# Scatters of one table in a two-layer transformer block: ordered behind the table's zeros instead of behind each other

## The chip, the cores and the metric

The kernel runs on one core of a Trainium2 chip. Time is what the device takes for one execution, in microseconds (us). Before the change it is 2133.94 us, the median of three runs (2133.84 to 2136.27). The program is built by a planner (the tile framework): the Python code names instructions in an order, the planner follows the reads and writes of tiles and tensors, decides in which order each engine issues its instructions, and places the semaphore waits.

## The reference, cut to what matters

Input x is (4, 1024, 128) in float32; it passes through two layers, each an attention-like part and a mixture of experts.

```
h = layernorm(x) * (1 + ca) + sa ;  x = x + ga * attention(h)       # layer 0: 16 heads, causal softmax
h = layernorm(x) * (1 + cb) + sb ;  x = x + gb * moe_top2(h)        # 8 experts, 2 per token
h = layernorm(x) * (1 + ca) + sa ;  x = x + ga * selective_scan(h)  # layer 1: state-space scan
h = layernorm(x) * (1 + cb) + sb ;  x = x + gb * moe_capacity(h)    # 8 experts, 512 places each
```

Both mixtures send a token to the experts that the router chose. The kernel does this with tables in device memory: rows of tokens are sorted by expert, an expert works on blocks of 128 rows, and results are fetched back by the same indices. Every token and choice has a row of its own in the table, so that two scatters never write the same row; unused rows have to be zero.

## The kernel before, in words

Tokens lie in 32 tiles of 128 (8 to a batch item b). Layer 0's attention runs in eight stages (b, c), c being one of two halves of the heads. A stage walks 8 query tiles i in the order 7, 0, 6, 1, 5, 2, 4, 3 (n = 0 to 7), each in four groups g of 32 queries: `probabilities` makes scores on TensorE (PE), subtracts the minimum on VectorE (DVE, line 567), exponentiates on ScalarE (ACT, line 580), takes the reciprocal of the sum (DVE, `den`, line 583) and scales by it on GpSimd (POOL, line 586). `turned` (line 595) then transposes these probabilities on PE, and `weighted` multiplies them by the values. Query tile i is transposed while tile n + 1 is made: `second_half`. POOL also zeroes the part over the diagonal (line 684) and adds the rotated halves of q and k (lines 537 and 545).

The layer-0 mixture of item b - 1 is put beside stages (b, 0) and (b, 1), in steps of Python generators. `sort_tokens` (stage (b, 0); two steps per group g from n = 2 on) norms, routes, computes each token's row (`placei`, DVE line 381), and then scatters 8 tiles times 2 choices = 16 tiles of 128 rows of 512 bytes into the table `f_in[b]`, named `blocks_in` in the profile (line 385). Stage (b, 1) runs `Blocks`: a load (line 407) brings three blocks, the experts' matmuls follow, results go to `blocks_out`, and `return_steps` gathers them (line 287). For the last item `sort_tokens` and `Blocks` run beside layer 1's scan, whose own chain is PE `pu` (spread), DVE `pu` (906), ACT `da` (908), DVE scan `h` (910), POOL `hc` (914), PE `py`. There are 16 steps m of this for each item, two `hc` each; `h` has 3 buffers.

Layer 1's mixture scatters 28 tiles into `xd` (`slots_in`, line 997), which the change leaves alone, and the last four tiles, in `dispatch_last`, as 8 scatters into the table `g_in` (line 1077). `last_experts` loads that one (line 1107).

All tables are filled with zeros at the start by transfers of SP's queue (line 491). Engines issue in order, and so do the queues of SP and POOL: an instruction that waits holds up everything behind it. A scatter is issued by POOL[...]. Since the rows of a scatter are not known when the program is built, the planner takes each for a write of the whole table: a scatter waits until the one before it into the same table has landed, and the load waits for the last. To choose what an engine does next, the planner runs its own model of time; of the instructions that are ready in it, the one written first in the Python code goes first.

Of the kernel before, what the change touches and what calls it, by code (L numbers as in the profile page):

```python
# [49 lines left out]
def adaln_two_layers(ctx: ExitStack, tc: tile.TileContext, I: dict, out: bass.AP):  # L50
    nc = tc.nc
# [10 lines left out]
    def load(pool, name, eng=nc.sync):  # L62
# [13 lines left out]
        out=causal, in_=causal, compare_op=ALU.is_ge, fill=NEG, base=0, pattern=[[-1, P]], channel_multiplier=1  # L76
# [219 lines left out]
            yield  # L296
        add()

    kept = {}

    hT0 = keep.tile([P, S + 3], F32, name="hT0")
    nc.gpsimd.memset(hT0[:, 0:3], 0.0)
# [28 lines left out]
    def sort_tokens(b, kept, pool, ps, tag, xtag="fxn"):  # L331


        xn = pool.tile([P, TB, D], F32, tag=xtag, bufs=1, name="fxn")
        yield from norm_steps(b * TB, TB, xn)
        hT = pool.tile([P, S], F32, tag=tag, bufs=1, name="fhT")
        yield from feature_steps(xn, hT, ps, modT[0][:, 4, b : b + 1], modT[0][:, 3, b : b + 1])
        pl = ps.tile([P, TB, NE], F32, tag="m", name="fpl")
        for t in range(TB):
            mm(nc, pl[:, t, :], hT[:, t * P : (t + 1) * P], f_gate)  # L340
        yield
        m1, m2, oh1, oh2 = yield from top2_steps(pl, sm)

        both = sm.tile([P, TB, NE], F32, tag="f_both", bufs=1, name="f_both")
        nc.vector.tensor_add(both, oh1, oh2)
        flat = both.rearrange("p t e -> p (t e)")
        pin = ps.tile([P, TB + 1, NE], F32, tag="m", name="fpin")
        pinf = pin.rearrange("p t e -> p (t e)")
        mm(nc, pinf[:, : TB * NE], before, flat, stop=False)
        for n in range(1, TB):  # L350
            mm(nc, pinf[:, n * NE : TB * NE], ones, flat[:, : (TB - n) * NE], start=False, stop=(n == TB - 1))
        mine = sm.tile([P, NE], F32, tag="f_mine", bufs=1, name="f_mine")
        nc.vector.tensor_reduce(mine, both.rearrange("p t e -> p e t"), AX.X, ALU.add)
        mm(nc, pin[:, TB, :], ones, mine)
        yield
        z = sm.tile([P, TB], F32, tag="f_z", bufs=1, name="f_z")
        nc.vector.scalar_tensor_tensor(z, m1, 1e-20, m2, ALU.add, ALU.add)
        nc.vector.reciprocal(z, z)
        w = keep.tile([P, 2, TB], F32, tag=f"f_w{b}", name="f_w")
        nc.vector.tensor_mul(w[:, 0], m1, z)  # L360
        nc.vector.tensor_mul(w[:, 1], m2, z)
        yield

        blocks, upto, which = yield from find_blocks(pin[:, TB, :], NB, sm)
        expert = keep.tile([P, NB], I32, tag=f"f_expert{b}", name="f_expert")
        nc.vector.tensor_scalar(expert, which, float(NE - 1), None, ALU.min)
        yield

        nc.vector.tensor_tensor(upto, upto, blocks, ALU.subtract)
        pos = sm.tile([P, TB, NE], F32, tag="f_pos", bufs=1, name="f_pos")  # L370
        nc.vector.scalar_tensor_tensor(
            pos, upto.unsqueeze(1).to_broadcast([P, TB, NE]), float(P), pin[:, :TB, :], ALU.mult, ALU.add
        )
        yield
        place = sm.tile([P, 2, TB], F32, tag="f_place", bufs=1, name="f_place")
        placei = keep.tile([P, 2, TB], I32, tag=f"f_placei{b}", name="f_placei")
        for k, oh in enumerate((oh1, oh2)):
            nc.vector.tensor_mul(oh, oh, pos)
            nc.vector.tensor_reduce(place[:, k], oh, AX.X, ALU.add)
            yield  # L380
        nc.vector.tensor_copy(placei, place)
        kept[b] = expert, placei, w
        for t in range(TB):
            for k in range(2):
                nc.gpsimd.indirect_dma_start(
                    out=f_in[b][:, :],
                    out_offset=bass.IndirectOffsetOnAxis(ap=placei[:, k, t : t + 1], axis=0),
                    in_=xn[:, t, :],
                    in_offset=None,
                )  # L390
                yield

    class Blocks:
# [9 lines left out]
        def load(self, n):  # L403
            rows_in = f_in[self.b].rearrange("(q p) d -> p q d", p=P)
            m = min(3, NB - 3 * n)
            self.xe = self.pool.tile([P, 3, D], F32, tag="fxe", name="fxe")
            nc.sync.dma_start(self.xe[:, :m], rows_in[:, 3 * n : 3 * n + m])

        def turn(self, n):

# [52 lines left out]
    with ExitStack() as es:  # L463
# [22 lines left out]

        for slots in f_in + xd + [g_in]:
            flat = slots.rearrange("(p r) d -> p (r d)", p=P)
            for at in range(0, flat.shape[1], 512):
                n = min(512, flat.shape[1] - at)  # L490
                nc.sync.dma_start(flat[:, at : at + n], mask[:, :n])

        def rotated(w, chunk, hT, dst):

# [242 lines left out]
    with ExitStack() as es:  # L737
# [273 lines left out]
        def dispatch_last():  # L1011
# [62 lines left out]
            yield  # L1074
            for t in range(nt):
                for k in range(2):
                    nc.gpsimd.indirect_dma_start(
                        out=g_in[:, :],
                        out_offset=bass.IndirectOffsetOnAxis(ap=placei[:, k, t : t + 1], axis=0),
                        in_=hx[:, t, :],  # L1080
                        in_offset=None,
                    )
                yield

            tiles = slice(t0, t0 + nt)
# [1 line left out]
                x[:, tiles, :], x[:, tiles, :], gate_bias[:, b : b + 1, :].to_broadcast([P, nt, D])  # L1087
            )

        sent = []  # L1090

        def last_experts():

            b, nb = B - 1, NLB
            expert = sent[0][0]
            rows_in = g_in.rearrange("(q p) d -> p q d", p=P)
            rows_out = g_out.rearrange("(q p) d -> p q d", p=P)
            ws, ins, xT, ye = {}, {}, {}, {}

            def load(j):  # L1100
                for r in range(j, min(j + 2, nb)):
                    ws[r] = load_block(eb, 6, "gw", "g_w", expert, r)

            def rows(q):
                n = min(4, nb - q)
                ins[q] = eb.tile([P, 4, D], F32, tag="gxe", name="gxe")
                nc.sync.dma_start(ins[q][:, :n], rows_in[:, q : q + n])

            def hidden(j):
                q = j - j % 4  # L1110
                if j == q:
                    n = min(4, nb - q)
                    tp = ps_m.tile([P, 4, P], F32, tag="m", name="gtp")
                    for r in range(n):
                        nc.tensor.transpose(tp[:, r], ins[q][:, r], ident)
                    xT[q] = eb.tile([P, 4, P], F32, tag="gxT", name="gxT")
                    shift, scale = modT[1][:, 3, b : b + 1], modT[1][:, 4, b : b + 1]
                    nc.vector.tensor_scalar(xT[q][:, :n], tp[:, :n], scale, shift, ALU.mult, ALU.add)
                    if q + 4 < nb:
                        rows(q + 4)  # L1120
                    ye[q] = eb.tile([P, 4, D], F32, tag="gye", name="gye")
                n = min(2, nb - j)
                ph = [ps_u.tile([P, NFC, P], F32, tag=f"pu{(j + r) % 4}", name="gph") for r in range(n)]
                act = eb.tile([P, 2, NFC, P], F32, tag="gact", name="gact")
                for r in range(n):
                    for f in range(NFC):
                        mm(nc, ph[r][:, f], ws[j + r][:, f * P : (f + 1) * P], xT[q][:, j - q + r])
                    nc.scalar.activation(act[:, r], ph[r], AF.Gelu_apprx_tanh)
                return j, n, act

            def results(j, n, act):
                q = j - j % 4
                py = ps_y.tile([P, 2, D], F32, tag="py", name="gpy")
                for r in range(n):
                    w = ws.pop(j + r)
                    for f in range(NFC):
                        w2 = w[:, NFC * P + f * D : NFC * P + (f + 1) * D]
                        mm(nc, py[:, r], act[:, r, f], w2, start=(f == 0), stop=(f == NFC - 1))
                nc.vector.tensor_mul(
                    ye[q][:, j - q : j - q + n], py[:, :n], gate_b1[:, b : b + 1, :].to_broadcast([P, n, D])  # L1140
                )
                if j + 6 < nb:
                    load(j + 6)
                if j > q or j + n == nb:
                    nc.scalar.dma_start(rows_out[:, q : j + n], ye[q][:, : j + n - q])

            rows(0)
            for j in range(0, 6, 2):
                load(j)
            made = None  # L1150
            for j in range(0, nb, 2):
                ahead = hidden(j)
                if made is not None:
                    results(*made)
                made = ahead
                yield
            results(*made)
# [274 lines left out]
```

## Time and profile before

| what | value |
|---|---|
| median of three runs | 2133.94 us |
| the profiled execution's own time | 2139.09 us |
| its span, first to last instruction | 2137.4 us |
| mean granted PE clock | 0.915 of full speed |
| PE busy | 1792.8 us (84%) |
| DVE busy | 1323.7 us (62%) |
| POOL busy | 994.6 us (47%) |
| scatters into `blocks_in` | 64, 986 ns each (median), from 490.2 us to 1581.5 us |
| scatters into `g_in` | 8, 957 ns each, from 1941.6 us to 1961.3 us |

A profile page gives each engine's busy time, then the same in forty slices, where a digit is the busy share in tenths. A view of one tile lists the instructions that touch it, with durations as least/median/most in ns, and for how long its engine sat idle before them and what ended that. A timeline gives start and duration of instructions in order; an idle time before an instruction stands in brackets with what ended it ("issue" where the profile shows nothing that was waited for). A view by stretches gives each engine's busy time between two moments, then PE's granted clock, the share of the DMA engines and GB/s.

### The profile page before, as it was taken

To read this page: it belongs to the slowest core of one execution; us is meant where nothing else is said; L and a number is where in the kernel's file an instruction comes from. 1 tells how busy PE (TensorE), PEld (TensorE's weight loads), DVE (VectorE), ACT (ScalarE), POOL (GpSimd) and SP (SyncE) were. 2 spreads that over 40 slices of the span, in tenths; PEclk is the share of its full clock that TensorE was granted. 3 is DMA by queue.
4 is the path that set the end of the run, shared out by engine and by line. 5 is a ranking of instruction groups with operands and counts; after the bars stand their busy time and mean duration, and the time that the engine had idled before them with its cause. 6 is when DMAs were issued, how large, how long until landed. Compare 5 with 4: busy or idle time off the path is not lost. (4 is left out here: it accounts for less than half of the span.)

```text
span 2137.4 us, 29054 instructions
## 1 busy us (share of the span) xinstructions
PE 1792.8 (84%) x8957; PEld 971.7 (45%) x8957; DVE 1323.7 (62%) x4000; ACT 947.3 (44%) x2073; POOL 994.6 (47%) x1277
## 2 busy tenths in 40 slices
PE   5399999998999989899989899967769757857984
PEld 3144344444455445455535446533335423325774
DVE  5356556665667666566766566655858888882243
ACT  1145454554445374355455454544456345423321
POOL 1334534436523643633363652344654675772254
PEclk9699999999999999999989999987979877867997
DMA  6400101001222200222210122210003230002345
GB/s 221 137 1 15 36 1 28 23 1 54 72 75 68 70 4 27 73 59 68 78 36 1 51 75 65 61 44 10 26 30 98 71 113 13 8 21 88 99 144 149
DMA packets 103756, 123.59 MB, mean 58 GB/s; under 512 B 15024, under 2 KB 68656, under 8 KB 103600
## 3 DMA queue, kind: packets, MB, share of 16 engines
q1 hardware_dynamic: 84256, 99.01, 15.7%
q0 software_dynamic: 8192, 16.74, 2.4%
q10 hardware_dynamic: 11152, 5.97, 0.9%
q8 instruction: 71, 1.16, 0.2%
q14 instruction: 85, 0.70, 0.1%
HBM read 67.85 MB, written 32.90 MB: 47 GB/s over the span
## 5 line engine op out<-in xcount | busy, mean ns | idle before, releaser
L586 POOL TENSOR_SCALAR pr<-pr,den 128x32 f32<-128x32 f32 (+31 forms) x512 | 353.2, 705 | 301.9 <-DVE den L583 295.9
L580 ACT ACTIVATE pr<-pr,nb 128x32 f32<-128x32 f32 (+31 forms) x512 | 371.6, 727 | 194.5 <-DVE nb L567 191.5
L595 PE MATMUL pt<-ident,pr 128*128 128x128 f32 x2304 | 341.9, 283 | 46.4 <-POOL pr L586 37.0
L46 PE MATMUL sc<-k,q 64*128 64x512 f32 (+14 forms) x1536 | 332.4, 525 | 41.4 <-DVE nb L567 24.4
L595 PEld LDWEIGHTS pt<-ident,pr 128*128 128x128 f32 x2304 | 253.8, 142 | 242.5 <-POOL pr L586 76.4
L46 PE MATMUL po<-pT,v 128*64 128x512 f32 x1152 | 345.9, 623 | 2.3 <-DVE pT L599 2.0
L597 ACT COPY pT<-pt 128x512 f32<-128x512 f32 x288 | 167.5, 582 | 356.8 <-PE pt L595 295.5
L567 DVE CUSTOM_DVE_ANT_0 pr<-sc,mask 128x512 f32<-128x512 f32 (+15 forms) x512 | 273.0, 559 | 76.2 <-PE sc L46 67.1
L599 DVE COPY pT<-pt 128x512 f32<-128x512 f32 x288 | 198.4, 689 | 166.1 <-PE pt L595 152.9
L46 PEld LDWEIGHTS sc<-k,q 64*128 64x128 f32 x1536 | 123.8, 193 | 197.6 <-DVE nb L567 93.3
L914 POOL TENSOR_TENSOR hc<-h,cc 128x512 f32<-128x512 f32 x128 | 161.6, 1275 | 108.7 <-DVE h L910 43.1
L46 PE MATMUL pu<-du,spread 128*128 128x512 f32 x256 | 146.4, 677 | 45.4 <-DVE h L910 41.0
L684 POOL MEMSET pr<- 128x288 f32 x128 | 42.4, 339 | 265.4 <-PE pt L595 261.3
L567 DVE CUSTOM_DVE_ANT_0 pr<-sc,mask,nb 128x416 f32<-128x416 f32 (+15 forms) x256 | 120.0, 496 | 7.0 <-PE sc L46 5.8
L908 ACT ACTIVATE da<-dt,negA 128x512 f32<-128x512 f32 x128 | 91.6, 719 | 66.1 <-DVE h L910 65.9
L46 PEld LDWEIGHTS po<-pT,v 128*64 128x64 f32 x1152 | 69.6, 136 | 84.4 <-issue 43.0
L503 DVE TENSOR_TENSOR rot_w<-proj,sin_sb 128x512 f32<-128x512 f32 x80 | 55.1, 688 | 76.7 <-PE proj L46 43.2
L906 DVE TENSOR_TENSOR pu<-pu,bb 128x512 f32<-128x512 f32 x128 | 85.2, 684 | 25.0 <-PE pu L46 14.9
L1300 POOL DMA_INDIRECT y<-slots_out,slot x56 | 56.5, 1009 | 93.8 <-PE ph L46 50.2
L46 PEld LDWEIGHTS pu<-du,spread 128*128 128x128 f32 x256 | 45.8, 207 | 115.4 <-DVE h L910 69.5
L545 POOL TENSOR_TENSOR q<-rot_u,rot_v 128x512 f32<-128x512 f32 x64 | 81.2, 1270 | 33.4 <-DMA rot_v<-rot_w 25.0
L580 ACT ACTIVATION_READ_ACCUMULATOR pr<-pr,nb 128x1 f32 x512 | 96.3, 188 | 0.0
(273 smaller groups left out, 2716.8 us busy)
## 6 DMA issues: line engine op xcount, KB each, us to landing
fw<-in_f_w SPq DMA_DIRECT2D x92, 320.0 KB
rot_v<-rot_w SPq DMA_DIRECT2D x320, 64.0 KB
gw<-in_g_w SPq DMA_DIRECT2D x15, 512.0 KB
fxe<-blocks_in SPq DMA_DIRECT2D x28, 192.0 KB
blocks_out<-fye SPq DMA_DIRECT2D x28, 192.0 KB
blocks_in<-mask SPq DMA_DIRECT2D x20, 256.0 KB
slots_in<-mask SPq DMA_DIRECT2D x16, 256.0 KB
g_w<-in_g_w SPq DMA_DIRECT2D x8, 512.0 KB
```

What stands on the lines that cost most here:

```text
L46: return nc.tensor.matmul(out, lhsT, rhs, start=start, stop=stop)
L545: nc.gpsimd.tensor_add(to, u.rearrange("p (n q) -> p n q", q=QG), v.rearrange("p (n q) -> p n q", q=QG))
L567: nc.vector.tensor_tensor_reduce(out=pr[hp][:, g, lo:hi], in0=sc[:, hp, : hi - lo], in1=mask[:, MW - hi + lo :] if hi == nk else mask[:, : ...
L580: nc.scalar.activation(p, p, AF.Exp, bias=nb[:, last, hp : hp + 1], scale=-1.0, accum_out=den[:, hp : hp + 1])
L586: nc.gpsimd.tensor_scalar(p, p, den[:, hp : hp + 1], 1.0, ALU.mult, ALU.mult)
L595: next_to(hp == 0 and g == 0, lambda: nc.tensor.transpose(to, p, ident))
L597: nc.scalar.copy(pT[:, hp, :], pt)
L599: nc.vector.tensor_copy(pT[:, hp, :], pt)
L906: nc.vector.tensor_mul(pu, pu, bb[:, tok])
L908: nc.scalar.activation(da, dt[:, tok], AF.Exp, scale=negA[:, c : c + 1])
L914: nc.gpsimd.tensor_mul(hcs[-1], h, cc[:, tok])
L1300: nc.gpsimd.indirect_dma_start(out=y, out_offset=None, in_=yd[k][:, :], in_offset=bass.IndirectOffsetOnAxis(ap=slot[:, k, t : t + 1], axis=0),
```

## The change

A function `scatter` now issues every scatter of `f_in[b]` and `g_in`. It keeps a list for each table. Its first entry is the name of a group; from the second scatter on, `declare_no_dep` takes away the waits for scatters that are in the group. Each scatter is then put into the group and given waits for the transfers that zero the table (`zeros`, six of them for an `f_in` table, four for `g_in`). `behind` gives each load of such a table a wait for every scatter into it, where before it waited for the last one. Computation, sizes, number of instructions and buffers are the same. The scatters into `xd` and all gathers are unchanged.

```diff
+    def after_all(ins, others, reason):
+        for other in others:
+            tc.add_manual_dep(ins, other.name,
+                mybir.DependencyInfo(mybir.DependencyClass.Sync, mybir.DependencyReason.DATA), reason=reason)
+
+    def scatter(group, out, at, in_, fill):
+        ins = nc.gpsimd.indirect_dma_start(
+            out=out, out_offset=bass.IndirectOffsetOnAxis(ap=at, axis=0), in_=in_, in_offset=None
+        ).ins
+        if group:
+            tc.declare_no_dep(ins, group=group[0], reason="different rows")
+        else:
+            group.append(f"rows of {ins.name}")
+        tc.add_to_no_dep_group(group[0], ins)
+        after_all(ins, fill, "zeros")
+        group.append(ins)
+
+    def behind(read, group):
+        after_all(read.ins, group[1:], "scattered rows")
...
         for t in range(TB):
             for k in range(2):
-                nc.gpsimd.indirect_dma_start(
-                    out=f_in[b][:, :],
...
+                scatter(arrived[b], f_in[b][:, :], placei[:, k, t : t + 1], xn[:, t, :], zeros[b])
...
-            nc.sync.dma_start(self.xe[:, :m], rows_in[:, 3 * n : 3 * n + m])
+            behind(nc.sync.dma_start(self.xe[:, :m], rows_in[:, 3 * n : 3 * n + m]), arrived[self.b])
...
         for slots in f_in + xd + [g_in]:
+            zeros.append([])
...
-                nc.sync.dma_start(flat[:, at : at + n], mask[:, :n])
+                zeros[-1].append(nc.sync.dma_start(flat[:, at : at + n], mask[:, :n]).ins)
...
-                    nc.gpsimd.indirect_dma_start(
-                        out=g_in[:, :],
...
+                    scatter(came_in, g_in[:, :], placei[:, k, t : t + 1], hx[:, t, :], zeros[-1])
...
-                nc.sync.dma_start(ins[q][:, :n], rows_in[:, q : q + n])
+                behind(nc.sync.dma_start(ins[q][:, :n], rows_in[:, q : q + n]), came_in)
```

More of the change, by code (lines that the diff above doesn't have):

```diff
@@ L297, in return_steps @@
         add()
-    kept = {}
+    def after_all(ins, others, reason):
+        for other in others:
+            tc.add_manual_dep(
+                ins,
+                other.name,
+                mybir.DependencyInfo(mybir.DependencyClass.Sync, mybir.DependencyReason.DATA),
+                reason=reason,
+            )
+    def scatter(group, out, at, in_, fill):
[11 more added lines that the diff above has]
+        after_all(read.ins, group[1:], "scattered rows")
+    kept, arrived, zeros = {}, {}, []
     hT0 = keep.tile([P, S + 3], F32, name="hT0")
@@ L382, in sort_tokens @@
         kept[b] = expert, placei, w
+        arrived[b] = []
         for t in range(TB):
             for k in range(2):
-                nc.gpsimd.indirect_dma_start(
-                    out=f_in[b][:, :],
[L387 to L390, printed above, removed]
+                scatter(arrived[b], f_in[b][:, :], placei[:, k, t : t + 1], xn[:, t, :], zeros[b])
                 yield
@@ L1076, in dispatch_last @@
                 for k in range(2):
-                    nc.gpsimd.indirect_dma_start(
-                        out=g_in[:, :],
[L1079 to L1082, printed above, removed]
+                    scatter(came_in, g_in[:, :], placei[:, k, t : t + 1], hx[:, t, :], zeros[-1])
                 yield
@@ L1088, in dispatch_last @@
             )
-        sent = []
+        sent, came_in = [], []
         def last_experts():
```

## The prediction

> **What bounds the kernel now.** I read the page first: shares, slices, and the chain that ended last.
>
> ```profile
> span 2137.4 us, 29054 instructions
> ...
> PE   5399999998999989899989899967769757857984
> ...
> POOL 1334534436523643633363652344654675772254
> PEclk9699999999999999999989999987979877867997
> ```
>
> PE is full through layer 0's attention (from the third slice to the 26th), so a microsecond in which PE stands there is a microsecond of the end. POOL is half idle: its own waits cost only where PE waits for POOL. The view of the table `blocks_in`, and then that of `g_in`, says what the scatters wait for:
>
> ```profile
> L385 POOL DMA_INDIRECT blocks_in<-fxn,f_placei x64: 966/986/1476, 490.2 to 1581.5; - x64
> ...
>   DMA blocks_in<-fxn,f_placei: 47.7, 34
>   issue: 4.5, 27
> ```
> ```profile
>   DMA g_in<-hx,g_placei: 13.0, 7
> ```
>
> So the waits that the change takes away are 47.7 us in 34 pieces, and 13.0 us in 7. By the timeline of POOL they lie in four windows of 16 scatters (from 490, 837, 1178 and 1530 us: 12.3, 13.3, 12.2 and 9.9 us) and one of 8 (from 1941 us). What they cost PE is read from the same place on both engines, here the second window; first POOL, then PE, then the view by stretches (length, then busy times of PE, PEld, DVE, ACT, POOL; clock):
>
> ```profile
> 864.99 0.98 POOL L385 DMA_INDIRECT blocks_in<-fxn,f_placei  x1 [1.16 <-DMA blocks_in<-fxn,f_placei]
> 867.50 0.97 POOL L385 DMA_INDIRECT blocks_in<-fxn,f_placei  x1 [1.54 <-DMA blocks_in<-fxn,f_placei]
> 868.49 1.28 POOL L537 TENSOR_TENSOR k<-rot_u,rot_v 128x512 f32<-128x512 f32 x1
> 869.72 1.52 POOL L586 TENSOR_SCALAR pr<-pr,den 128x608 f32<-128x608 f32 x2
> ```
> ```profile
> 870.56 0.48 PE L595 MATMUL pt<-ident,pr 128*128 128x128 f32 x1 [5.80 <-POOL pr L586]
> ```
> ```profile
> 524.00:530.00 6.00, 6.00 (x17) 3.25 (x17) 1.12 (x4) 0.00 (x0) 4.37 (x5) 0.62 0.07 22
> ...
> 871.00:876.00 5.00, 4.71 (x17) 2.55 (x15) 1.44 (x4) 0.00 (x0) 4.25 (x6) 0.77 0.06 21
> ```
>
> The scaling of width 608 is late because POOL spent its time waiting for scatters to land: its `den` was there at 863.4 us (DVE, 863.17 + 0.17), it ran at 869.7. PE stood for 5.80 us, and afterwards ran at 0.77 of its clock for 5 us. The first and third windows show the same at the same scaling: 6.47 us (to 523.96) and then 0.62 for 6 us; 4.83 us (to 1221.54) and then 0.71 for 5 us.
>
> **The change part by part.**
>
> *Waits of the three attention windows.* A landing takes 2.51 us from one issue to the next where nothing lies between (`g_in`, 1944.15 to 1946.65), and 0.96 of it is the instruction, so 1.55 us is saved a time. A rule would make it less: the Trainium skill, "DMA: Bandwidth & Descriptors", section on the anatomy of a GpSimd DMA, has 2.0 us fixed plus bytes over 436e3 a us; 64 KB give 2.15, less 0.96 is 1.19 (an estimate from that page), or 40 us for 34 waits. The trace has 47.7 and I take that.
>
> POOL then has to do all its work without gaps. The price of a scatter is not zero: twelve gathers in a row (2070 to 2085 us) take 1.30 us apiece, 1.00 and 0.30 of issue, and scatters into `slots_in` between other work 1.01 and 0.17. What matters is how much earlier the scaling 608 comes. Window 2: from the first scatter (837.5) 10.1 us of waits lie before it and 12 scatters; if the other 4 now also go ahead of it that costs 4 x 1.3 = 5.2, and denser issue about 1.0 more: 3.9 us earlier, PE's stall 5.80 becomes 1.9. If they don't go ahead, `den` is the limit and the whole 5.80 is gained. Window 1: 10.8 - 5.2 - 1.0 = 4.6 of 6.47. Window 3: 14 scatters are ahead already, 12.2 - 2.6 - 1.2 = 8.4, more than the stall, so 4.83. I take the lower ends, 4.6 + 3.9 + 4.8 = 13.3.
>
> *The clock.* After the three stalls PE lost 6 x 0.38 + 5 x 0.23 + 5 x 0.29 = 4.9 us of full-speed time. By the skill, "TensorE: Matmul & The Clock Gate", Part 1, the clock halves after an idle window of some 3.4 us and a window of activity raises it: that would be 3 x 1.7 = 5.1 us lost now. It also says that stalls cut to 1.9 us are safe, which no row here shows; by the row alone I could claim only a share equal to that of the stall removed (13.3 of 17.1, 3.8 us). I take 4.9. Attention: -18.2 us. PE is full right afterwards (1.00 of 1.00 busy from 537 to 560), so this goes through to the end.
>
> *The fourth window* is another matter. POOL was itself the bound from 1530.1 to 1551.4: 9 `hc` of 1.27 (11.4 us), 8 scatters, some 2.2 us of waits, and PE's `py` waits for the last `hc` (5.28 us, 1551.40). By the code all 16 scatters stand at steps m up to 12, and POOL is at m = 12 to 15 by then: freed, all are overdue, and are taken before the `hc`. Then 16 x 1.29 + 11.4 = 32.1 us instead of 21.3: +10.8. Against it: the 7 scatters that now follow to 1581 are out of the way, and PE may do the next item's inputs (`p`, `pd`, ready from 1547, done at 1559) before `py`, at best -10. The nearest row is the trace's own bunch:
>
> ```profile
> 1748.10 0.95 POOL L287 DMA_INDIRECT fy<-blocks_out,f_placei  x1 [0.30 <-issue]
> 1749.07 3.70 POOL L914 TENSOR_TENSOR hc<-h,cc 128x512 f32<-128x512 f32 x3
> ```
> ```profile
> 1744.94 2.08 PE L46 MATMUL pu<-du,spread 128*128 128x512 f32 x2 [13.26 <-DVE h L910]
> ```
>
> Sixteen overdue gathers from 1728.07 to 1749.05 went ahead of `hc` whose `h` was done by 1730.5, and PE stood for 13.26 us. There was less other work for PE than at 1551. Nearer to the upper end, I take +4.
>
> *`g_in`*: 0. POOL has nothing from 1962.3 to 2012.5, PE is full of slot experts, and the table's blocks are first transposed at 2065.5; the load was issued at 1963.6. Without that 100 us of cover its 13.0 us would count in full. SP's order could put the load before an `xe` load; with four `xe` buffers ahead that is within -0 and +1. I take 0.
>
> *New waits*: zeros landed by some 70 us, 420 us before the first scatter: 0; uncovered they would be one landing, 2.5 us. Loads wait for 16 scatters: semaphore instructions on SP of 17 to 28 ns (26 of them for these loads now), at most seven more a table, 5 x 7 x 0.028 = 1 us on SP's queue. Behind them wait the rotations (`rot_v`), POOL's additions of q after those; the first load is needed at 554.4 and goes out at 543.8, so 0, up to +1 if it blocks `rot_v` at the wrong moment. The load cannot be later: the last scatter is earlier. Transfers in flight together: 16 x 64 KB in 21 us are 50 GB/s, where the last slices carry 149: 0.
>
> **Sum**: -18.2 + 4 = -14.2. The profiled execution took 2139.09 (span 2137.4, 1.7 around it), 5.1 above the median; on the span 2123.2, on the median 2133.94 - 14.2 = **2119.7 us**.
>
> **The rivals.**
>
> *The burst (slower).* The planner is free to issue scatters as soon as `placei` is there, and POOL works in order: where its model shows an idle moment, it puts scatters ahead of scalings that on the chip are ready. A burst of 8 ahead (10.3 us) delays the scalings of n = 5 in windows 1 and 2 to about 505 (500.6 + 4.7; PE needs them at 503.8: +1.5 each) and in window 3 the scaling 736 to 1190.8 (PE got it at 1187.35: +3.5). That makes -18.2 + 6.5 + 10.8 = -1: this is the point from which it decides. With all 16 ahead, PE stands 11.8, 11.8 and 13.8 us longer there, -18.2 + 37.4 + 10.8 = +30. At 12, half way, +15: 2149 us. For it: the bunch at 1728, and POOL idle for 2.56 us right before the first scatter at 1178.75. Against: the scalings of n = 5 stand ahead of scatters 4 to 15 in the code, and were ready in a row (x3 between scatters), so the planner takes them first.
>
> *Hidden (same).* PE's order is new everywhere, another producer (`den` behind `rot_w` on DVE, at 875.46 now) ends the same stall, the fourth window costs 10.8: -18.2 halved and +10.8, 2135.6 us.
>
> *The waits stay.* If the declaration did not reach the scatters, the time would be 2133.9. All pieces are in the code; little speaks for it.
>
> **How the numbers follow.** Gain as summed 0.58 (its own range 2107 to 2129, from full stalls and -10 in the fourth window to half the attention gain); burst 0.25 (2138 to 2164); hidden 0.14; waits stay 0.03. No change means within 0.2%, 4.3 us, about what a measurement of this kernel can tell. Faster 0.58; hidden and stay, less a part of hidden that ends above, 0.16; slower 0.26. The range reaches over both signs: 2107 to 2150 leaves out one in ten of the burst's upper part and about as much below.
>
> **What would show it.** The view of `blocks_in` and `g_in` has no idle time behind their own DMA. The scaling 608 follows its `den` at once, and the three PE stalls of 4.8 to 6.5 us shrink below 2 with the clock at 1.00 behind them; spans of the three windows fall from 50, 49 and 48 us to about 44 for the same matmuls. In the scan, 16 scatters stand in a row at 1.29 us before the last `hc`, and `py` is later than its neighbours on PE. It would be wrong if scalings (line 586) ready for long stand behind rows of scatters in the attention windows, or if other stalls have appeared outside the five windows from a new order of all engines.

## The result, and the profile after

The changed kernel takes 2149.24 us (median of 4, 2148.12 to 2151.59), the kernel before on the same chip 2135.11 us (median of 4, 2133.84 to 2139.17). The ratio is 1.0064, with a 95% interval of 1.0047 to 1.0082: slower by 0.6%, where 0.7% less had been forecast. (The number lies just inside the range of 2107 to 2150 us, which the slow rival had widened; the forecast was a gain.) The profiled execution took 2151.59 us, its span is 2149.9 us (before: 2137.4).

The waits did go. First the views of the two tables `blocks_in` and `g_in` after the change (of 64 and 8 scatters). Their own landing does not appear any more among what POOL was idle for; 47.7 us and 13.0 us stood there.

```profile
L311 POOL DMA_INDIRECT blocks_in<-fxn,f_placei x64: 967/972/1213, 491.1 to 1556.7; - x64
...
  issue: 16.4, 60
...
who waited for it (us, times):
  ACT fxn L172: 7.5, 1
```
```profile
L311 POOL DMA_INDIRECT g_in<-hx,g_placei x8: 957/962/962, 1953.8 to 1962.6; - x8
...
  DVE g_placei L1096: 4.8, 1
  issue: 2.1, 7
```

(L311 is the scatter, now in the function `scatter`; other lines of the file moved by 24 or so: 586 is 610, 684 is 708, 914 is 938.) The first view's last line is new: an activation on ACT waits 7.5 us for scatters.

The page's mean clock is 0.915, as before, and PE is busy 84% of the span, as before. So the loss has to be looked for in who waits for whom. What PE waited for, before and then after (us in total, times, longest):

```profile
PE pu L46 <- DVE h L910: 41.0, 25, 13.3
PE pt L595 <- POOL pr L586: 37.0, 38, 6.5
PE py L46 <- POOL hc L914: 30.7, 14, 9.3
PE sc L46 <- DVE nb L567: 24.4, 51, 1.8
PE pt L595 <- ACT pT L597: 5.4, 10, 1.4
```

```profile
PE py L46 <- POOL hc L938: 45.8, 16, 10.1
PE sc L46 <- DVE nb L591: 28.6, 51, 4.5
PE pu L46 <- DVE h L934: 28.4, 23, 6.9
PE pt L619 <- POOL pr L610: 23.5, 36, 5.7
PE pt L619 <- ACT pT L621: 11.6, 11, 6.1
```

PE does wait 13.5 us less for the scalings on POOL, nearly the 13.3 us that the prediction subtracted, and 12.6 us less for `h`. But it waits 15.1 us more for `hc`, 6.2 us more for the copies `pT` on ACT, and 4.2 us more for `nb`. The timeline of POOL in the second window tells why:

```profile
849.87 0.59 POOL L610 TENSOR_SCALAR pr<-pr,den 128x384 f32<-128x384 f32 x1
851.19 1.05 POOL L311 DMA_INDIRECT blocks_in<-fxn,f_placei  x1 [0.17 <-issue]
...
861.48 0.97 POOL L311 DMA_INDIRECT blocks_in<-fxn,f_placei  x1 [0.30 <-issue]
862.43 0.36 POOL L708 MEMSET pr<- 128x288 f32 x1
```

Nine scatters stand in a row, from 851.19 to 862.45 us, ahead of a memset of 0.36 us. That memset zeroes the part over the diagonal of the probabilities of the next query tile. Two instructions on DVE and PE answer to it:

```profile
862.83 0.28 DVE L591 CUSTOM_DVE_ANT_0 pr<-sc,mask,nb 128x64 f32<-128x64 f32 x1 [4.71 <-POOL pr L708]
```
```profile
864.68 2.08 PE L46 MATMUL sc<-k,q 64*128 64x512 f32 x4 [4.53 <-DVE nb L591]
```

The masked pass of DVE writes into what the memset clears, so it waits 4.71 us, and PE waits 4.53 us behind it. The first window has the same row of nine, 502.13 to 513.40; there PE's stall behind DVE is 1.70 us, and 2.15 us more follow. The scaling of width 608, which the prediction wanted 4.6 us earlier there, starts at 524.83 us, 1.7 us *later* than before (523.13), though no scatter has been waited for.

In the third window six scatters go ahead of the scalings of width 768, and then ACT's normalization of the scan's first item, which before ran behind the last scatter of this window, has been put between the copies of this window, some 19 us earlier. Its destination is the buffer `fxn` that the scatters still read. PE first, then ACT, after and before:

```profile
1192.91 1.36 PE L619 MATMUL pt<-ident,pr 128*128 128x128 f32 x5 [5.67 <-POOL pr L610]
...
1210.87 1.97 PE L619 MATMUL pt<-ident,pr 128*128 128x128 f32 x8 [6.11 <-ACT pT L621]
```
```profile
1209.47 0.88 ACT L172 ACTIVATE fxn<-x,ln_away,ln_r 128x128 f32<-128x128 f32 x2 [7.52 <-DMA blocks_in<-fxn,f_placei]
```
```profile
1228.75 0.50 ACT L172 ACTIVATE fxn<-x,ln_away,ln_r 128x128 f32<-128x128 f32 x1
```

In the scan, twelve scatters in a row run from 1536.27 us until 1551.35, then one `hc`, four more scatters, and the other eight `hc`. PE's `py` waits 10.09 us for the first of them; the same matmuls before (second view) stood behind nothing. The 5.28 us that the prediction read at 1551.40 stood before a later `py`, which now runs at 1567.77 without a wait:

```profile
1552.70 1.94 PE L46 MATMUL py<-hc,gather 128*32 128x512 f32 x8 [10.09 <-POOL hc L938]
```
```profile
1535.50 1.07 PE L46 MATMUL py<-hc,gather 128*32 128x512 f32 x8
```

Matching the same matmuls in both traces, the changed kernel stands at +0.2 us before the first window, +3.4 behind it (first expert block), +2.8 at the routing of the second item, +1.3 behind the second window, +8.5 at the end of layer 0, +6.2 at the start of the scan, +13.0 at the last table `g_in` and +12.5 at the end. There are two losses, of about 7 us in the third window and about 7 us in the scan, and no gain in the first two windows.

### The profile page after: what moved, and what is told of

Same layout as the page of the kernel before. It is cut to its first block, busy times and chain, and to the rows that moved or that the text cites. A ratio compares the mean times of both kernels' runs of the same rounds, so it can differ in the third digit from the quotient of the medians.

```text
span 2149.9 us, 29066 instructions
## 1 busy us (share of the span) xinstructions
PE 1798.7 (84%) x8957; PEld 966.8 (45%) x8957; DVE 1332.7 (62%) x4000; ACT 948.2 (44%) x2073; POOL 995.8 (46%) x1277
## 5 line engine op out<-in xcount | busy, mean ns | idle before, releaser
L46 PE MATMUL sc<-k,q 64*128 64x512 f32 (+14 forms) x1536 | 337.4, 531 | 47.4 <-DVE nb L591 28.6
L46 PE MATMUL pu<-du,spread 128*128 128x512 f32 x256 | 154.6, 710 | 43.1 <-DVE h L934 28.4
```

Source lines behind the costliest of these rows:

```text
L46: return nc.tensor.matmul(out, lhsT, rhs, start=start, stop=stop)
```

## The experiments

The theory after this reading: the freed waits are worth what was forecast, but a freed scatter may also be *issued* at another place, and the planner put rows of scatters ahead of short POOL instructions that others need, and changed the order of the other engines with it (**order**). The first rival: sixteen transfers of one table under way together are slow, or their writing disturbs others (**in flight**). The second: each window pays for something else, as the buffer `fxn` or the longer list of waits of a load. Times of one batch share a chip: for the first four runs the kernel before has there a median of 2122.97 us, for the next four 2123.04, for the next three 2121.57, for the last 2135.49. Ratios are compared, not times; the expectations in us were written for the kernel before at 2134. Traces of another chip compare with that of before only roughly. The kernel with `g_in` alone issues everything on PE, DVE, ACT and POOL in the order of before and keeps all other waits, yet its trace stands at -7.6 us at the end of layer 0 and at -16.4 at the last table; the one with the scan's table alone and the order kept, unchanged in layer 0, stands there at +0.6.

### The two halves of the change apart

One kernel has the change's waits, with all engines' instructions held to the order that they had before, by constraints on the order of issue that place no semaphore. The other has the order of the changed kernel and the waits of before.

```diff
+    free = {i.name for g in [*arrived.values(), came_in] for i in g[1:]}
+    for steps in ast.literal_eval(zlib.decompress(base64.b85decode(ORDER)).decode()).values():
+        last, among = None, []
+        for n in itertools.accumulate(steps):
+            ins = nc.find_inst_by_name("I-%d" % n)
...
+            for to in ([] if ins.name in free else among) or [last]:
+                if to is not None:
+                    tc.add_manual_dep(ins, to,
+                        mybir.DependencyInfo(mybir.DependencyClass.NoSync, mybir.DependencyReason.DATA),
+                        reason="order of issue")
```

(`ORDER` lists the instructions of the kernel before, engine by engine. In the second kernel it lists those of the changed one, put into the code of before.)

> The change's waits (scatters behind the zeros only), but every engine issues its instructions in the order of the kernel before; only neighbouring scatters may swap. Order theory (the loss is the planner's new order, the freed waits by themselves are a gain): about 2117 us, since the three stalls of PE at the scaling of width 608 (17.1 us) shrink to a few us, and about 2 us go in the scan. In-flight theory (several scatters under way at once are slow by themselves, in POOL's issue or in landing): 2135 us or more. Nothing-to-gain theory (POOL's waits were hidden, PE finds another wait at once): 2130 to 2138 us.

> The waits of the kernel before (each scatter behind the one before it), but every engine in the order of the kernel after. Order theory: clearly slower than the kernel after, since rows of up to 12 scatters that stand ahead of POOL's other work now take 2.5 us apiece instead of 1.3: 2170 to 2220 us. In-flight theory: no slower than the kernel after, 2149 us or less.

The order kept: 2100.59 us, ratio **0.9892** (0.9876 to 0.9907). The new order with the old waits: 2203.83 us, ratio **1.0370** (1.0355 to 1.0385). With the waits of the change alone the kernel is 1.1% faster; by the order of the change alone it is 3.7% slower. In the traces PE, DVE, ACT and POOL do issue in the order that was to be held. The gain is larger than the 2117 us expected (0.992); the loss lies within the 2170 to 2220 us. The two don't add up: the order costs 3.7% with the old waits and less without them. From the order kept to the change is 1.0064 - 0.9892 = 1.7%, some 37 us, which is the price of the order once the waits are gone. The view of `blocks_in` with the order kept (its scatters are line 418 there, since the list of the order takes lines):

```profile
L418 POOL DMA_INDIRECT blocks_in<-fxn,f_placei x64: 963/982/1212, 488.8 to 1554.0; - x64
...
  issue: 11.9, 57
...
DMA to landing us min/median/max: 2.2/2.4/8.1
```

No waits for the table's own transfers here either; the median from issue to landing is 2.4 us. With the old waits, where only one is under way, it is 2.3 us. (This view counts the table's loads and zeros too; for the 64 scatters alone it is 2.3 and 2.2 us.) So a landing is not slower, and the kernel is faster. Nor are sixteen under way: at one scatter every 1.28 us and 2.3 us to land, it is about two at a time, in a long row too. In flight falls for such rows as this order has; in the changed kernel's own trace the landings of these scatters are not recorded, but with rows of five (a run below) the median is 2.3 us as well.

### The tables apart

> Only the three tables scattered beside attention are freed; the fourth and g_in keep their waits. By the two traces, layer 0 ends 6 to 8 us later than before: order theory 2140 to 2143 us. If the loss came from the scan or from new order elsewhere: 2133 to 2136 us. My prediction's sum for these windows: 2117 us.

> Only the table scattered beside the scan is freed. The step of my prediction (16 overdue scatters go ahead of the hc) put it at +4, between -10 and +10.8; by the two traces the first scan item ends 4.4 us later and the rest of the scan adds 2: 2139 to 2142 us. If all the loss is in attention: 2134 to 2136 us.

> Only g_in is freed, the other four tables wait as before. GpSimd's 13.0 us of waits there go; the prediction had 0 us for it because 100 us of other work cover it: ratio 1.000 (0.999 to 1.001). If the landing of g_in were on the path after all, 0.994 to 0.998.

```diff
         if group:
-            tc.declare_no_dep(ins, group=group[0], reason="different rows")
+            if fill is not zeros[-1] and fill is not zeros[B - 1]:
+                tc.declare_no_dep(ins, group=group[0], reason="different rows")
```

(This is the edit for the attention tables; for the scan's table alone the condition is `fill is zeros[B - 1]`, for `g_in` alone `fill is zeros[-1]`. All three leave the order to the planner.) The three attention tables alone: 2129.64 us, 1.0021 (1.0003 to 1.0039). The scan's table alone: 2134.90 us, 1.0050 (1.0038 to 1.0063). `g_in` alone: 2122.30 us, 1.0007 (0.9996 to 1.0017). The first two add up to 0.71%, which is the change's 0.64% within the intervals. `g_in` is worth nothing, as forecast, although its waits are gone. Neither part gains when the planner orders it anew. In us the first was expected at 2140 to 2143 (1.003 to 1.004), which its interval meets; the second at 2139 to 2142 (1.002 to 1.004), which it exceeds.

### The same two parts with the order kept

> The order of before held on every engine, and only the three attention tables freed: the prediction's term for the attention windows by itself, with the scatters where it had them. The prediction said -18.2 us, which is 0.9914 of 2123. If the first experiment's gain (0.9892) is the sum of the attention windows and of the fourth one, with the share that the sixth run leaves for the fourth: 0.9925 (0.991 to 0.9945). If all of the gain is in the attention windows: 0.989.

> The order of before held on every engine, and only the scan's table freed: 2.2 us of GpSimd's waits lie before the last hc there, 7.7 us behind it. If the loss of the fourth experiment (1.005) is the order's and not the table's, this is faster than before: 0.9965 (0.995 to 0.9985). If the freed table costs whatever the order, 1.003 to 1.006; if it is hidden, 1.000.

```diff
         if group:
-            tc.declare_no_dep(ins, group=group[0], reason="different rows")
+            if fill is not zeros[-1] and fill is not zeros[B - 1]:
+                tc.declare_no_dep(ins, group=group[0], reason="different rows")
```

(This stands beside the block of the first experiment, which holds the order of every engine; for the scan's table the condition is again `fill is zeros[B - 1]`.) The attention tables: 2104.54 us, **0.9913** (0.9892 to 0.9934). The scan's table: 2121.56 us, **0.9995** (0.9981 to 1.0009). The expectation of 0.9965 for the scan's table missed: there the gain of the waits is hidden. A cost of holding the order as such does not show either. So the attention tables are worth 0.87% in the old order and cost 0.2% in the planner's; the scan's is worth nothing in the old one and costs 0.5% in the planner's. The second window of POOL with the attention tables free and the order kept (scalings are line 718 here, memsets 816):

```profile
850.13 1.47 POOL L718 TENSOR_SCALAR pr<-pr,den 128x576 f32<-128x576 f32 x2 [0.64 <-DVE den L715]
851.77 1.06 POOL L418 DMA_INDIRECT blocks_in<-fxn,f_placei  x1 [0.17 <-issue]
852.82 0.64 POOL L816 MEMSET pr<- 128x288 f32 x2
853.63 0.98 POOL L418 DMA_INDIRECT blocks_in<-fxn,f_placei  x1 [0.17 <-DMA rot_v<-rot_w]
854.92 0.97 POOL L418 DMA_INDIRECT blocks_in<-fxn,f_placei  x1 [0.30 <-DMA rot_v<-rot_w]
855.91 1.29 POOL L669 TENSOR_TENSOR k<-rot_u,rot_v 128x512 f32<-128x512 f32 x1
857.16 1.53 POOL L718 TENSOR_SCALAR pr<-pr,den 128x608 f32<-128x608 f32 x2
```

Scatters stand one or two between the others' instructions, the scaling 608 runs at 857.16 us (before: 869.72), and POOL now waits for `den`, not the reverse. The stretches around the scaling, in the columns of the prediction's view (length, busy times of PE, PEld, DVE, ACT, POOL, then the clock), first before, then the change, then attention tables free and order kept; in each the second line is the third window. They are the same stretches of time, not quite of work: by the third window the last kernel is some 14 us ahead.

```profile
845.00:877.00 32.00, 25.34 (x123) 12.49 (x119) 15.49 (x51) 10.03 (x23) 21.35 (x27) 0.89 0.15 42
1183.00:1223.00 40.00, 32.35 (x166) 16.33 (x165) 19.54 (x66) 17.92 (x45) 26.78 (x36) 0.94 0.12 35
```
```profile
845.00:877.00 32.00, 27.48 (x134) 13.28 (x131) 14.53 (x47) 11.31 (x24) 24.25 (x31) 0.89 0.19 56
1183.00:1223.00 40.00, 28.14 (x132) 14.85 (x134) 13.05 (x45) 16.42 (x43) 24.54 (x34) 0.79 0.11 34
```
```profile
845.00:877.00 32.00, 29.39 (x130) 12.58 (x130) 20.14 (x59) 13.19 (x32) 24.43 (x29) 1.00 0.26 68
1183.00:1223.00 40.00, 37.86 (x184) 17.69 (x182) 25.20 (x72) 18.70 (x44) 25.97 (x33) 1.00 0.22 59
```

In the order kept PE is busy for 29.39 of 32 us and for 37.86 of 40, at 1.00 of its clock in these stretches. In the change PE gains 2 us in the second window at the same clock of 0.89, and loses 4 us and 0.15 of clock in the third.

### What in the order costs: POOL, the others, the buffer, the number in flight

Only POOL's order kept: the block of the first experiment, with a list of POOL's instructions alone.

```diff
+    for steps in ast.literal_eval(zlib.decompress(base64.b85decode(ORDER)).decode()).values():
```

> The change's waits with only GpSimd's order held to that of before; the other engines get whatever order the planner then gives them (TensorE's differs from before in 433 places). If GpSimd's order alone is the cause, most of the first experiment's gain comes back: 0.989 to 0.994. If the new order of the other engines costs by itself: 0.998 to 1.006.

The scatters of the attention tables in the program's order, the other two tables as before:

```diff
-        ins = nc.gpsimd.indirect_dma_start(
+        dma = nc.gpsimd.indirect_dma_start(
...
-            tc.declare_no_dep(ins, group=group[0], reason="different rows")
+            if fill is not zeros[-1] and fill is not zeros[B - 1]:
+                tc.declare_no_dep(ins, group=group[0], reason="different rows")
...
+        if fill is not zeros[-1] and fill is not zeros[B - 1]:
+            tc.keep_in_program_order(dma)
```

> Only the three attention tables are freed, and each of their scatters is kept where the program has it among GpSimd's instructions that the planner orders; the scan's table and g_in keep their waits. Theory of the order (rows of scatters ahead of the scalings are the cost): the rows are 3, 1, 2, 5 ahead of the memset of pr instead of 9, and TensorE has the order of before, so most of the attention windows' gain of the first experiment is there: ratio 0.992 to 0.996. If only the exact order of before gains, or if three in flight and more are themselves slow, 1.000 to 1.003, like the third experiment (1.0021).

The same for the scan's table too, with all tables free:

```diff
+        if fill is not zeros[-1]:
+            tc.keep_in_program_order(dma)
```

> The change with the scatters of all four attention and scan tables kept where the program has them among GpSimd's instructions; g_in is free. It differs from the sixth run (0.9928) by the scan's table being freed. In the kernel itself the planner's row of 12 scatters ahead of hc is then bound by the program's order. If the program's order serves the scan as it served the attention windows: 0.991 to 0.993. If the new order that the planner gives the scan costs what the fourth experiment showed (1.005 for that table alone): 0.996 to 0.999.

The change with another buffer for the norm of the scan's items:

```diff
-            xn = ab.tile([P, TB, D], F32, tag="fxn", bufs=1, name="fxn")
+            xn = ab.tile([P, TB, D], F32, tag="xn", bufs=1, name="fxn")
```

> The change, with the norm of the scan's items (first_features) in the buffer of the other norms (xn) instead of that of the attention items (fxn), so that ScalarE's norm no longer has to wait for the scatters that read fxn. In the third window that wait was 7.52 us on ScalarE and stood 6.11 us before a matmul of TensorE. If the forward move of this norm costs as the trace reads, about 6 us of 2149 go: ratio to before 1.0035 (1.002 to 1.005) instead of 1.0064. If ScalarE's wait only takes the place of another (the scaling 768 behind 8 scatters, 5.67 us just before it), the ratio stays at 1.006.

The change with at most two scatters of a table under way:

```diff
-            tc.declare_no_dep(ins, group=group[0], reason="different rows")
+            tc.declare_no_dep(ins, group=group[0], keep=group[1:][-2:-1], reason="different rows")
+            after_all(ins, group[1:][-2:-1], "two in flight")
```

> Each scatter waits for the one two before it, so that at most two of a table are on their way; the planner orders all engines anew and knows of the wait, and its rows of scatters are then 4 at most instead of 9 and 12. If the rows' length ahead of GpSimd's other work is the cost: between the change and the order of before, 0.996 to 1.002. If any new order of all engines costs as the change's does, 1.004 to 1.008.

What they measured:

| kernel | time us | ratio to before (95%) |
|---|---|---|
| the change, only POOL's order kept | 2111.71 | 0.9951 (0.9933 to 0.9968) |
| attention tables free, their scatters in the program's order | 2106.16 | 0.9928 (0.9914 to 0.9943) |
| attention and scan tables and `g_in` free, scatters of the first four in the program's order | 2137.21 | 1.0007 (0.9997 to 1.0018) |
| the change, the scan's norm in another buffer | 2129.08 | 1.0035 (1.0023 to 1.0046) |
| the change, two of a table in flight at most | 2134.65 | 1.0055 (1.0033 to 1.0077) |

**POOL's order** alone brings 1.0064 - 0.9951 = 1.1% of the 1.7% back; it lies just above what was expected (0.989 to 0.994), so an order of the other engines made anew has a price of its own, 0.6%. The traces place it in the scan. Up to 1586 us PE and DVE issue in the order of before here, though nothing holds them to it, and only ACT's norm has moved; at the end of layer 0 this kernel stands at -18.8 us against before, the one with every order kept at -21.4, which is less apart than two chips can be. From there to the last table it moves by +1.2, while the five kernels that keep the order of the scan move by -1.7 to -8.8. So in the attention windows the new order of PE and DVE follows from POOL's; what it costs there by itself was not separated. In the scan the others' order costs some 3 to 10 us more, by these single traces.

**The program's order** serves the attention windows: 0.9928 against 0.9913 in the order of before. PE and DVE keep the order of before throughout. Its rows ahead of the memset are five long instead of nine (500.52 to 506.68), and one long stall is left, 6.63 us at 1174.72 behind six scatters in the third window. With the scan's table freed too, the same line is worth nothing: 1.0007, just above the 0.996 to 0.999 expected of the dearer case. Keeping the program's order does not break up the row in the scan, since the order in which the program names them has the scatters there in a row; the row begins at 1525.83; its last, and PE:

```profile
1539.95 0.97 POOL L311 DMA_INDIRECT blocks_in<-fxn,f_placei  x1 [0.30 <-issue]
1540.95 1.27 POOL L941 TENSOR_TENSOR hc<-h,cc 128x512 f32<-128x512 f32 x1
```
```profile
1542.28 1.93 PE L46 MATMUL py<-hc,gather 128*32 128x512 f32 x8 [10.11 <-POOL hc L941]
```

It also seems to have lost most of the attention gain: -4.1 us at the end of layer 0, where the run with the attention tables alone has -17.2. That is not the order: up to 1511 us PE, DVE, ACT, POOL and SP's transfers are in the same order in both, and from 480 us on PE's stalls in layer 0 are of the same length, within 1.1 us each. What differs is the granted clock, 0.94, 0.94 and 0.89 from 480 to 560, 820 to 900 and 1160 to 1240 us, against 0.98, 0.98 and 0.96. Why it differs, between two chips and with the same stalls, is open; and 1.0007 is 0.3% more than 0.9928 and the 0.50% of the scan's table make.

**The buffer** `fxn` was worth 1.0064 - 1.0035 = 0.3%, some 6 us, as its 6.11 us stall reads. The 5.62 us stall behind six scatters in the third window remains, and the 6.11 us one is gone (the planner now puts this norm ahead of the window, at 1156.6). So the third window's ACT wait is shown to be one of the two causes there.

**Two in flight** did not help: 1.0055, above the 0.996 to 1.002 expected if the rows' length were all. Its rows are four at most, but POOL runs the scaling 608 at 524.60 us, 1.5 us later than before, and PE stands for 7.98 us at it (7.02 in the second window). Not the scatters hold it up: the last was issued at 515.07. POOL stood for the rotated half `rot_v`, and SP's queue had the first load of the table, which waits for all scatters, ahead of its transfers. POOL, then SP's queue:

```profile
523.37 1.26 POOL L562 TENSOR_TENSOR k<-rot_u,rot_v 128x512 f32<-128x512 f32 x1 [5.18 <-DMA rot_v<-rot_w]
```
```profile
518.25 0.92 SPq L431 DMA_DIRECT2D fxe<-blocks_in  x2
519.29 0.56 SPq L533 DMA_DIRECT2D rot_v<-rot_w  x1
```

Before, `rot_v` went out at 510.97 us and that load at 543.8, behind it. In the changed kernel the load stands ahead of `rot_v` too (516.32 and 519.50 us), but `rot_w`, from which it is made, comes only at 518.74 us there. So this run has a price of order of another kind, and doesn't tell what the length of a row is worth.

## Why the prediction was wrong, step by step

**Waits of the attention windows, with the clock (-18.2 us).** As a price of the waits this was right: the attention tables alone, with the order of before, give 1 - 0.9913 = 0.87% of 2121.57, 18.5 us (0.9892 to 0.9934: 14 to 23). The trace stands at -18.4 us at the end of layer 0, closer than traces of two chips agree. The parts are not those of the sum. The three windows gave 8.9, 9.3 and 6.0 us, 24.2 together, where 6.9, 5.1 and 6.2 were put (the stall's share of the clock with it), and 5.8 us were given back between the windows, most of it from 560 to 820 us, where its clock is 0.97 (before: 0.99). That the sum fits is in part luck. The lower ends were too low for an order that stays: no further scatters went ahead of the scaling 608, and its whole stall went in all three windows, as the upper ends had it. On the clock the row and the rule of the Trainium skill ("TensorE: Matmul & The Clock Gate", Part 1) had 3.8 and 5.1 us. With the order kept, no PE stall in the windows reaches 2 us, and the clock is 1.00 in the first two (480 to 540 and 836 to 880 us), but 0.94 in the third (1160 to 1220). The page names idle gaps above some 3.4 us; that shorter ones are safe, as the prediction read it, the runs do not bear out. With the attention tables in the program's order a stall of 1.70 us, at 522.07, is followed by a clock of 0.66 (columns as above):

```profile
522.00:527.00 5.00, 4.82 (x16) 2.31 (x17) 1.98 (x7) 2.42 (x6) 0.78 (x2) 0.66 0.38 93
```

**The step that failed** is in the same paragraph, and in the rival that was to guard it: "if the other 4 now also go ahead of it" took the rest of POOL's order as given, and of the burst it was said that "the scalings of n = 5 stand ahead of scatters 4 to 15 in the code, and were ready in a row (x3 between scatters), so the planner takes them first". The scalings of n = 5 did stay between the scatters (rows of three, one and two). But then came a row of nine, ahead of a memset of 0.36 us that no step of the prediction had named, and DVE, then PE, wait for it. The prediction costed the scatters against one consumer, the scaling 608; the change freed them against all. The runs price this: 1.0021 with the planner's order against 0.9913, so 1.1% or 23 us of the attention tables.

**The burst**, at 0.25, was the rival that came true, and its case of 12 scatters ahead had 2149 us, but not by its working, so that the number agrees is luck: it put the price on the scalings of n = 5 in the first two windows, where PE did not stand for them. Only its third window is as it said, 5.67 us instead of 2.27 at the scaling 768 (it had +3.5 at eight scatters ahead, and called the scaling 736, which PE got earlier; there were six). Beside it stands what it did not have: ACT's norm, moved forward by some 19 us into a buffer that the scatters read.

**The fourth window (+4 us between -10 and +10.8).** The sign was right, and so was the mechanism of 16 overdue scatters ahead of the `hc`: twelve and four of them. POOL's sum came true, although it counted 8 scatters ahead of the last `hc` and 7 behind where the trace has 7 and 9: that `hc` starts at 1566.5 us, before at 1550.1, and of these 16.4 us 6.2 were there at the start of the scan, so 10.2 where 10.8 were put. Other work of PE covers a part, as was said: the next item's first matmuls of `dg` start at 1581.61, before at 1570.94, 4.5 us net where +4 was taken. But the term ends there. With the planner's order the table costs 0.50%, 10.6 us, near the upper end; the rest is lost after that item, with another order on all engines, and which move costs it is open. With the order kept the table is worth nothing (0.9995), so the waits there were hidden.

**`g_in` (0 us), new waits (0 us).** Right for this change: 1.0007 for `g_in` alone, with 0.9996 to 1.0017 around it. The longer lists of waits of the loads are in the kernel with the order kept too, and that is 1.1% faster, so they cannot cost much in that order. The "+1 if it blocks `rot_v` at the wrong moment" was too small a bound: with two in flight the load that blocked `rot_v` cost PE 7.98 us.

**"PE's order is new everywhere"**, said of the hidden case, was half of the truth: in the scan it costs some 3 to 10 us by itself, in the attention windows it follows from POOL's. The chance of 0.58 for the gain rested on a sum over waits; nothing in it priced a free choice of the planner, though the prediction had seen that choice in the scan and applied it there only.

The best kernel measured is the change with the order of before, 0.9892 (0.9876 to 0.9907) of the time before. The one of few lines is the attention tables alone with their scatters in the program's order: 0.9928 (0.9914 to 0.9943).

## What to carry to other kernels

A dependency that is taken away is two changes: a wait less, and a place in the order set free. Price the second by asking of every short instruction on the same engine who would wait for it if all freed work stood ahead of it, and hold the order when the freed work is on an engine that others lean on. To judge such a change, run it once with the old order and once with the new order and the old waits: here the two halves were -1.1% and +3.7%, and the +0.6% of both together said nothing of either. And before a difference between two traces is put down to order, compare the order itself and the clock.

## What the runs showed of the hardware that was not expected

Scatters of 64 KB from POOL, issued one after another without a wait, follow each other every 1.28 us, against 2.51 us when each waits for the one before to land, and the landing is hardly slower for it (medians of the scatters from issue to landing of 2.3 and 2.2 us). No contention with PE's work showed: PE reached 1.00 of its clock and 29.39 busy us of 32 while the DMA engines carried more than before (68 GB/s instead of 42 in that stretch).

The granted clock cost more than the stalls tell: two kernels with the same order and the same PE stalls in layer 0, on two chips, ended it 13.1 us apart, at clocks of 0.89 to 0.94 and of 0.96 to 0.98 around the windows, and stalls of 1.67 and 1.85 us were followed by clocks of 0.57 (527 to 531 us) and 0.66 (868 to 873) in one of them.
